# Layer 0 of a four-layer convolution stack: PSUM in two-bank tiles with one reader each, and a 128-column stationary for one image half

## The chip, the core and the metric

The kernel runs on one core of a Trainium2 chip. A core has TensorE (PE: matmuls, with the loading of stationary operands shown as PEld), VectorE (DVE), ScalarE (ACT), GpSimd (POOL, used here mostly to issue stores) and SyncE (SP, used to issue loads). Matmuls write PSUM, which has eight banks of 512 fp32 values in each of 128 partitions; ACT and DVE read PSUM and write SBUF. The metric is the device time of one execution in microseconds: 6857.07 us, the median of three runs (6852.17 to 6867.05).

## What is computed

The input x has the shape (4, 64, 256, 256) in fp32. Four layers follow one another, each of the form `x = x + conv(group_norm(x))`. Only layer 0 is touched:

```python
x = jnp.einsum('bchw,oc->bohw', x, w_in)            # 64 -> 384 channels
xp = x.reshape(B, C, H // p, p, W // p, p)...       # patches of 8 x 8
xp = irfft2(rfft2(xp) * fft_filter)                 # per channel and patch
x = conv_general_dilated(x, w_dw, 3 x 3, depthwise)
x1, x2 = jnp.split(x, 2, axis=1)
x = gelu(x1) * x2
return jnp.einsum('bchw,oc->bohw', x, w_out)        # 192 -> 64 channels
```

Layers 1 to 3 are a 3x3 convolution, a gated 1x1 convolution and a spectral convolution.

## The kernel before

Layer 0 treats the 64 pixels of a patch as the partition index of what it computes. The FFT filter and the depthwise 3x3 convolution are folded, at the start, into per-channel matrices from the 64 pixels of a patch (and of its right, lower and lower-right neighbours) to the pixels of an output patch. The image is cut into 12 blocks `p` of up to 12 patch rows, three per image; each block is worked in four channel blocks `kb` of 96 expanded channels (48 for each side of the gate). For each `kb` three kinds of work run on TensorE:

- Expansion, `expand(p, kb, t)`, once for each patch row `t` (11 or 12 of them; 544 tiles in the whole kernel). SBUF tile `xn` holds a normalised patch row: input channels of the left image half on partitions 0 to 63, of the right half on 64 to 127. A patch's 64 channels x 64 pixels are the stationary operand and the weights `win` (96 columns) the moving one, so the pixels come out on partitions and the channels along the free axis. `k` and `m` count eight pairs of patches, `s` the image half, `odd` the patch of a pair: 32 matmuls of 64x64 with 96 columns. The even patch of a pair goes to partitions 64 to 127 and the odd one to 0 to 63, with `win` read from column 48 or 0, so that one copy of 128 partitions can move both gate sides. The result is read by two ACT copies (L452, L455) and two DVE copies (L456, L457) into the big SBUF tile `u`.
- Convolution, `convolve(p, kb, g)`, twelve per `kb` (576 in all): per-channel matmuls of the folded matrices `w` with `u`, first 64x64 ones (L488), then 64x16, 64x28 and 64x4 ones (L497) that accumulate the neighbours' part. ACT applies Gelu to the first gate side (L504), DVE multiplies by the second (L505), POOL stores the product to DRAM (`gs`).
- Projection, `project(p - 1, r)`, for the block before: `g` is loaded back with channels on partitions and multiplied by `w_out` (L588 with 128x64, L595 with 64x64 tiles); DVE adds the residual `rt` (L603, L605) and takes the statistics for the next group norm (L611), POOL stores (L615). Eight units `r` per block; one runs after the expansions of each `kb` and one in the middle of its convolutions. `unit()` calls `project`, then `load_unit` for the next `r`.

All of layer 0's PSUM comes from `quad`: two tiles of four banks, used in turn by the three kinds of work and by the small matmuls of the group norms:

```python
def quad(name):
    return pp.tile([128, 4, 512], F32, tag=f"p{next(turn) % 2}", name=name)
```

The order on TensorE, ACT, DVE and SP is the order in which the program issues the work (`tc.manual_schedule`); a tile is reused when all its readers are done. The weights `w` are loaded by `load_w` into a ring of three tiles, two ahead. The other loads on SP are the next block's input rows, the statistics of the next image and the projection's operands. The constants `c_ident`, `c_avg32` and `c_sel32`, which only later layers read, are loaded at the very start.

Of the kernel before, what the change touches and what calls it, by code (L numbers as in the profile page):

```python
# [17 lines left out]
C = 64  # L18
HID = 192
# [102 lines left out]
class _Net:  # L122
    def __init__(self, ctx, tc, a):
# [10 lines left out]
        self.ident = self.load("c_ident")  # L134
        self.avg = self.load("c_avg")
        self.avg32, self.sel32 = self.load("c_avg32"), self.load("c_sel32")
# [30 lines left out]
    def stats_tile(self, name, n):  # L167

        return self.sp.tile([128, self.H // 2, 6], F32, tag="bst", name=name)[:, 0:n]
# [107 lines left out]
    def _layer0(self, ctx, dst):  # L277
# [5 lines left out]
        def quad(name):  # L283

            return pp.tile([128, 4, 512], F32, tag=f"p{next(turn) % 2}", name=name)

        self.small = lambda name: quad(name)[:, 0, :]
# [23 lines left out]
        p_w, p_h = pool("l0w", 3), pool("l0h", 4)  # L311
# [122 lines left out]
        def expand(p, kb, t):  # L434

            b, i0 = blocks[p]
            ps = quad(f"psu_{p}_{kb}_{t}")
            xn = xns[b, i0 + t]
            for k in range(2):
                for m in range(4):  # L440
                    for s in range(2):
                        for odd in range(2):
                            nc.tensor.matmul(  # L443
                                ps[halves[1 - odd], 2 * s + k, 2 * PB * m : 2 * PB * (m + 1)],
                                xn[halves[s], 2 * (4 * k + m) + odd].rearrange("p r w -> p (r w)"),
                                win[halves[s], kb, PB * (1 - odd) : PB * (3 - odd)], start=True, stop=True,
                            )
            v = ps[:, :, 0 : 8 * PB].rearrange("p s (m c) -> p c s m", m=4)
            n = 4 * 4
            at = lambda h, o: u[h, :, t * CW + o : t * CW + o + n].rearrange("p c (s m) -> p c s m", s=4)  # L450
            first, second = v[:, 0:PB], v[:, PB : 2 * PB]
            nc.scalar.copy(at(slice(0, 128), 1), first)  # L452
            lo, hi = halves
            k = PB * 7 // 12
            nc.scalar.copy(at(hi, E2 + 1)[:, 0:k], second[lo, 0:k])  # L455
            nc.vector.tensor_copy(at(lo, O1), second[hi])  # L456
            nc.vector.tensor_copy(at(hi, E2 + 1)[:, k:], second[lo, k:])  # L457
# [21 lines left out]
        def convolve(p, kb, g):  # L479

            ps = quad(f"pc_{p}_{kb}_{g}")
            G = NG * kb + g
            w = wl[p * (HID // 8) + G // 2]
            out = lambda lo, m, k, h: ps[lo : lo + m, 2 * k + h, 0:L].rearrange("p (i x j) -> p i x j", i=NR, x=2)
# [18 lines left out]
            v = ps.rearrange("p (k h) n -> p h k n", h=2)[:, :, :, 0:L]  # L503
            nc.scalar.activation(h, v[:, 0], AF.Gelu)  # L504
            nc.vector.tensor_mul(h, h, v[:, 1])  # L505
# [51 lines left out]
        def load_unit(p, r):  # L557
            if p < 0 or p >= NB:
                return
            load_r(p, r)  # L560
            for half in range(2):
                load_g(p, r, half)

        def project(p, r):
# [4 lines left out]
            po = quad(f"po_{p}_{r}")  # L569
            rt = rts.pop((p, r))  # L570
# [12 lines left out]
            for half in range(2):  # L583
                g1, g6 = loads.pop((p, r, half))
                for k in range(2):
                    for x in range(2):
                        for s in range(2):
                            nc.tensor.matmul(  # L588
                                out(2 * half + k, s, x), wo1, moving(g1[:, 2 * k], 2 * half + k, s, x),
                                start=(x == 0), stop=False, skip_group_check=True,  # L590
                            )
                for x in range(2):
                    for k in range(2):
                        for s in range(2):
                            nc.tensor.matmul(  # L595
                                out(2 * half + k, s, x), wo6[halves[k]],
                                moving(g6[halves[k], 0], 2 * half + k, s, x),
                                start=False, stop=True, tile_position=(k * C, s * C), skip_group_check=True,
                            )
            rv = rt.rearrange("p i (j w) -> p w (i j)", w=P)  # L600
            pv = po[:, :, 0 : 2 * n].rearrange("p b (k n) -> p b k n", k=2)
            v = rv[:, 1:7].rearrange("p (b k) n -> p b k n", k=2)
            nc.vector.tensor_add(v, v, pv[:, 0:3])  # L603
            v = bass.AP(tensor=rv.tensor, offset=rv.offset + 7, ap=[rv.ap[0], [-7, 2], rv.ap[2]])
            nc.vector.tensor_add(v, v, pv[:, 3])  # L605
# [28 lines left out]
        with ordered:  # L634
# [30 lines left out]
            for j in range(2):  # L665
                load_w(j)
# [19 lines left out]
            for p in range(NB + 1):  # L686
                units = iter(range(P if p > 0 else 0))
# [5 lines left out]
                for r in range(ahead):  # L693
                    load_unit(p - 1, r)

                def unit():
                    r = next(units, None)
                    if r is None:
                        return
                    project(p - 1, r)  # L700
                    if r + ahead < P:
                        load_unit(p - 1, r + ahead)

                if p == NB:
                    for r in range(P):
                        unit()
# [771 lines left out]
```

## Time and profile before

| What | Value |
|---|---|
| median of three runs | 6857.07 us |
| profiled execution, its own time | 6889.14 us |
| span of the profiled execution | 6887.4 us |
| mean granted TensorE clock | 0.938 |
| PE busy | 5931.4 us (86%) |
| DVE busy | 3944.2 us (57%) |
| ACT busy | 2973.2 us (43%) |
| POOL busy | 1049.0 us (15%) |
| last store of layer 0 issued | about 4315 us after the start |

A group line of the profile reads: source line, engine, operation, output and inputs by the program's names, for matmuls the stationary's rows and columns, shapes, count; then busy time in us and the mean of one in ns; then the engine's idle time just before these instructions and what ended most of it. A timeline line gives the start and length in us, and in square brackets the idle time before it and its releaser. A window line gives a stretch, its length, the busy time and number of instructions of PE, PEld, DVE, ACT and POOL, the granted TensorE clock (1.00 is full), the share of the DMA engines and GB/s. An fp32 matmul appears as two weight loads and two matmuls (two passes). The ends of matmuls are modelled; their starts are records.

### The profile page before, as it was taken

The numbers are of one execution on the slowest core, as the hardware profiler recorded it, in microseconds if no ns is written. First come the engines' busy times: TensorE is split into PE (matmuls) and PEld (weight loads), VectorE is DVE, ScalarE is ACT, GpSimd is POOL, SyncE is SP. The second block draws the span as 40 slices with busy tenths as digits, with TensorE's granted clock in tenths as the row PEclk, the third lists the DMA queues.
The fourth block names the chain that finished last, engine by engine and source line by source line (L and its number), as shares of the span: only waits on it lengthen the run. The fifth ranks groups of instructions, "written<-read, shape, count | busy, mean of one in ns | idle before, by whom it ended". The sixth has DMA issues, their size and how long they took to land.

```text
span 6887.4 us, 252749 instructions
## 1 busy us (share of the span) xinstructions
PE 5931.4 (86%) x115416; PEld 3078.3 (45%) x115416; DVE 3944.2 (57%) x4436; ACT 2973.2 (43%) x3172; POOL 1049.0 (15%) x1646
## 2 busy tenths in 40 slices
PE   2888888888888888888888886999989999999987
PEld 1444444444444444444444443333344444444476
DVE  5444444444444444444444443899888889886355
ACT  3332323233323233323333330677777777774211
POOL 3111111111111111111111111111112222221011
PEclk9999999999999999999999997999999999999855
DMA  7577878786878777878676769999957667667889
GB/s 223 147 195 195 216 200 213 198 204 196 216 202 213 196 210 198 212 197 216 190 201 185 193 175 223 240 229 227 227 134 175 167 173 173 177 168 250 330 341 391
DMA packets 878558, 1448.60 MB, mean 210 GB/s; under 512 B 77252, under 2 KB 586452, under 8 KB 875444
## 3 DMA queue, kind: packets, MB, share of 16 engines
q1 hardware_dynamic: 725284, 923.09, 53.6%
q0 software_dynamic: 148672, 500.14, 21.5%
q8 instruction: 909, 14.89, 1.0%
q10 hardware_dynamic: 3536, 9.20, 0.5%
q14 instruction: 157, 1.29, 0.1%
HBM read 932.08 MB, written 500.04 MB: 208 GB/s over the span
## 4 chain that ended last, share of the span: by engine, by line
PE 66%; DMA 14%; ACT 6%; DVE 5%; issue 5%; SPq 4%; POOL 0%; ACTq 0%; DVEq 0%; POOLq 0%
PE pc L497 13%; PE m L863 10%; PE pc L488 9%; PE psu L443 8%; PE one L1104 8%; PE div L1063 6%; DMA w<-wt 4%; DMA g<-g 4%; PE po L588 3%; ACT u L452 3%; DMA x<-x 2%; PE psz L1093 2%; SPq L544 2%; PE po L595 2%; ACT u L455 2%
## 5 line engine op out<-in xcount | busy, mean ns | idle before, releaser
L443 PE MATMUL psu<-win,xn 64*64 64x96 f32 x34816 | 934.2, 260 | 495.1 <-DVE u L457 303.6
L504 ACT ACTIVATE h<-pc 128x748 f32<-128x748 f32 x576 | 457.1, 794 | 2033.6 <-PE pc L497 2033.6
L505 DVE TENSOR_TENSOR h<-h,pc 128x748 f32<-128x748 f32 x576 | 535.8, 931 | 1273.9 <-ACT h L504 1273.9
L497 PE MATMUL pc<-u,w 64*16 64x374 f32 (+2 forms) x27648 | 1263.1, 489 | 0.7 <-issue 0.7
L443 PEld LDWEIGHTS psu<-win,xn 64*64 64x64 f32 x34816 | 842.5, 144 | 606.8 <-issue 254.0
L488 PE MATMUL pc<-u,w 64*64 64x374 f32 x9216 | 896.9, 498 | 119.3 <-DMA w<-wt 88.8
L456 DVE COPY u<-psu 64x768 f32<-64x768 f32 x544 | 522.0, 960 | 687.7 <-ACT u L455 637.5
L497 PEld LDWEIGHTS pc<-u,w 64*16 64x16 f32 (+2 forms) x27648 | 415.8, 93 | 788.6 <-issue 787.8
L452 ACT COPY u<-psu 128x768 f32<-128x768 f32 x544 | 461.7, 849 | 668.6 <-PE psu L443 664.5
L508 POOL DMA_DIRECT2D g<-h x576 | 416.1, 722 | 1728.7 <-DVE h L505 1636.8
L1049 DVE TENSOR_TENSOR q<-xn 128x2313 f32<-128x2313 f32 (+2 forms) x256 | 627.9, 2495 | 1.7 <-ACT xn L258 1.7
L1104 PE MATMUL one<-z,wp 32*32 32x512 f32 x16384 | 595.1, 597 | 21.1 <-issue 17.7
L488 PEld LDWEIGHTS pc<-u,w 64*64 64x64 f32 x9216 | 325.4, 134 | 623.8 <-issue 483.8
L258 ACT ACTIVATE xn<-x,nb,r 128x1024 f32<-128x1024 f32 (+3 forms) x272 | 485.5, 1788 | 180.9 <-DMA x<-x 142.8
L1050 ACT ACTIVATE q<-q 128x2313 f32<-128x2313 f32 (+2 forms) x256 | 529.0, 2086 | 30.0 <-DVE q L1049 29.0
L1063 PE MATMUL div<-q,ones 64*32 64x512 f32 x8192 | 474.0, 602 | 12.2 <-ACT q L1050 9.3
L1104 PEld LDWEIGHTS one<-z,wp 32*32 32x32 f32 x16384 | 368.6, 103 | 228.7 <-issue 86.9
L615 POOL DMA_DIRECT2D x<-r x192 | 148.4, 777 | 1872.7 <-DVE r L605 1555.1
L1137 POOL DMA_DIRECT2D x<-r x512 | 274.8, 545 | 981.1 <-DVE r L1134 965.9
L588 PE MATMUL po<-g,wo 128*64 128x176 f32 (+1 forms) x3072 | 315.3, 348 | 97.1 <-DMA g<-g 56.9
L603 DVE TENSOR_TENSOR r<-r,po 128x1056 f32<-128x1056 f32 (+1 forms) x96 | 198.1, 2064 | 321.1 <-PE po L595 295.8
L863 PE MATMUL m<-t,wk 64*64 64x512 f32 x3072 | 341.1, 588 | 0.0
(155 smaller groups left out, 6009.5 us busy)
## 6 DMA issues: line engine op xcount, KB each, us to landing
g<-h POOLq DMA_DIRECT2D x576, 374.0 KB, 7.5
x<-x SPq DMA_DIRECT2D x240, 640.0 KB, 6.5
w<-wt SPq DMA_DIRECT2D x288, 448.0 KB, 8.3
x<-x SPq DMA_DIRECT2D x100, 1024.0 KB, 14.1
g<-g SPq DMA_DIRECT2D x414, 187.0 KB, 5.9
g<-g SPq DMA_DIRECT2D x736, 93.5 KB, 5.8
x<-in_x_dram SPq DMA_DIRECT2D x256, 256.0 KB, 9.5
x<-o POOLq DMA_DIRECT2D x128, 512.0 KB, 8.4
```

The source lines that it names most:

```text
L443: nc.tensor.matmul(ps[halves[1 - odd], 2 * s + k, 2 * PB * m : 2 * PB * (m + 1)], xn[halves[s], 2 * (4 * k + m) + odd].rearrange("p r w -> ...
L452: nc.scalar.copy(at(slice(0, 128), 1), first)
L456: nc.vector.tensor_copy(at(lo, O1), second[hi])
L488: nc.tensor.matmul(out(C * c, C, k, h), w[halves[h], k, 2 * (G % 2) + c, 0:C], cells(h, 4 * g + 2 * k + c, 0, 0), start=True, stop=False, ...
L497: nc.tensor.matmul(out(q, m, k, h), w[halves[h], k, 2 * (G % 2) + c, c0 : c0 + m], cells(h, 4 * g + 2 * k + c, down, right), start=False, ...
L505: nc.vector.tensor_mul(h, h, v[:, 1])
L588: nc.tensor.matmul(out(2 * half + k, s, x), wo1, moving(g1[:, 2 * k], 2 * half + k, s, x), start=(x == 0), stop=False, skip_group_check=True,)
L863: nc.tensor.matmul(rows2(m)[halves[j], s], w[dx][halves[s]], ts[n][halves[s], i, 2 * j : 2 * j + 2, dx : dx + W], start=(dx == 0), stop=(d ...
L1049: nc.vector.tensor_sub(d, p0, p1)
L1050: nc.scalar.activation(d, d, AF.Square)
L1063: ins = nc.tensor.matmul(ps[quarters[j], h], ones[halves[h]], q[n, g, k][halves[h], r + 2 * j : r + 2 * j + 2, o : o + W], start=(m == 0), ...
L1104: ins = nc.tensor.matmul(rows2(ps[g])[quarters[j], k], w[quarters[i]], z[quarters[i], h, 2 * j + dy : 2 * j + dy + 2, dx : dx + W], tile_p ...
```

## The change

PSUM in layer 0 becomes four tiles of two banks (`banks`) in place of two of four. An expansion takes two of them: the left image half fills one, which only ACT reads (four copies of 64 partitions), the right half the other, which only DVE reads (three copies). For the left half, the two patches of a pair form one stationary of 64 rows and 128 columns; the right half keeps its 64x64 matmuls. The two kinds alternate: one of the first, two of the second, eight times. A convolution takes two tiles, one for each `k`, and Gelu and product are issued for each. A projection unit is cut into two halves of one tile each, run after the convolutions 1, 4, 7 and 10 of a `kb`; loads follow by halves (`load_half`). The ring of `w` has four tiles, loaded three ahead. The statistics tile is shorter, three constants are loaded after layer 0, and the group-norm step after the last convolution of a `kb` is skipped. The core of the diff:

```diff
-        def quad(name):
-            return pp.tile([128, 4, 512], F32, tag=f"p{next(turn) % 2}", name=name)
-        self.small = lambda name: quad(name)[:, 0, :]
+        def banks(name):
+            return pp.tile([128, 2, 512], F32, tag=f"p{next(turn) % 4}", name=name)
+        self.small = lambda name: banks(name)[:, 0, :]
...
-        p_w, p_h = pool("l0w", 3), pool("l0h", 4)
+        p_w, p_h = pool("l0w", 4), pool("l0h", 4)
...
         def expand(p, kb, t):
-            ps = quad(f"psu_{p}_{kb}_{t}")
+            ps = [banks(f"psu_{p}_{kb}_{t}_{s}") for s in range(2)]
+            lo, hi = halves
+            both = win[lo, kb, 0 : 2 * PB]
             for k in range(2):
                 for m in range(4):
-                    for s in range(2):
-                        for odd in range(2):
-                            nc.tensor.matmul(
-                                ps[halves[1 - odd], 2 * s + k, 2 * PB * m : 2 * PB * (m + 1)],
-                                xn[halves[s], 2 * (4 * k + m) + odd].rearrange("p r w -> p (r w)"),
-                                win[halves[s], kb, PB * (1 - odd) : PB * (3 - odd)], start=True, stop=True,
-                            )
...
+                    n, at = 2 * (4 * k + m), slice(2 * PB * m, 2 * PB * (m + 1))
+                    nc.tensor.matmul(
+                        ps[0][:, k, at], xn[lo, n : n + 2].rearrange("p n r w -> p (n r w)"), both, start=True, stop=True
+                    )
+                    for odd in range(2):
+                        nc.tensor.matmul(
+                            ps[1][halves[1 - odd], k, at], xn[hi, n + odd].rearrange("p r w -> p (r w)"),
+                            win[hi, kb, PB * (1 - odd) : PB * (3 - odd)], start=True, stop=True,
+                        )
...
-            nc.scalar.copy(at(slice(0, 128), 1), first)
-            nc.scalar.copy(at(hi, E2 + 1)[:, 0:k], second[lo, 0:k])
-            nc.vector.tensor_copy(at(lo, O1), second[hi])
-            nc.vector.tensor_copy(at(hi, E2 + 1)[:, k:], second[lo, k:])
+            for h, o, k, c in ((lo, O1, lo, 0), (hi, O2, lo, PB), (lo, E1 + 1, hi, 0), (hi, E2 + 1, hi, PB)):
+                nc.scalar.copy(at(h, o), v[0][k, c : c + PB])
+            nc.vector.tensor_copy(at(slice(0, 128), 8 + 1), v[1][:, 0:PB])
+            nc.vector.tensor_copy(at(hi, 8 + E2 + 1), v[1][lo, PB:])
+            nc.vector.tensor_copy(at(lo, 8 + O1), v[1][hi, PB:])
...
-            nc.scalar.activation(h, v[:, 0], AF.Gelu)
-            nc.vector.tensor_mul(h, h, v[:, 1])
+            for k in range(2):
+                nc.scalar.activation(h[:, k], ps[k][:, 0, 0:L], AF.Gelu)
+                nc.vector.tensor_mul(h[:, k], h[:, k], ps[k][:, 1, 0:L])
...
-        def project(p, r):
+        def project(p, r, half):
-            po = quad(f"po_{p}_{r}")
+            po, rt = banks(f"po_{p}_{r}_{half}"), rts[p, r]
...
-                    unit()
                     for g in range(NG):
-                            load_w(p * (HID // 8) + G // 2 + 2)
+                            load_w(p * (HID // 8) + G // 2 + 3)
                         convolve(p, kb, g)
-                        self.next_norms()
-                        if g == NG // 2:
+                        if g < NG - 1:
+                            self.next_norms()
+                        if g in (1, 4, 7, 10):
                             unit()
...
     net.layer0(x1)
+    late = ctx.enter_context(tc.tile_pool(name="late", bufs=1))
+    net.ident, net.avg32, net.sel32 = (net.load(name, late) for name in ("c_ident", "c_avg32", "c_sel32"))
```

## The prediction

> **What bounds the kernel now.** I read the groups by cost first, then the timeline of one expansion and one convolution stage, then the granted clock by window, and last the start records of all matmuls. "Slower" and "faster" below mean by more than 0.2%, about what a measurement of this kernel tells from no change.
>
> Layer 0 lasts to about 4312 us. Its rows:
>
> ```profile
> L443 PE MATMUL psu<-win,xn 64*64 64x96 f32 x34816 | 934.2, 260 | 495.1 <-DVE u L457 303.6
> L497 PE MATMUL pc<-u,w 64*16 64x374 f32 (+2 forms) x27648 | 1263.1, 489 | 0.7 <-issue 0.7
> L456 DVE COPY u<-psu 64x768 f32<-64x768 f32 x544 | 522.0, 960 | 687.7 <-ACT u L455 637.5
> L452 ACT COPY u<-psu 128x768 f32<-128x768 f32 x544 | 461.7, 849 | 668.6 <-PE psu L443 664.5
> L488 PE MATMUL pc<-u,w 64*64 64x374 f32 x9216 | 896.9, 498 | 119.3 <-DMA w<-wt 88.8
> ```
>
> The 544 expansion tiles (L443, two records per fp32 matmul) wait for their readers; the convolutions (L488, L497) wait for almost nothing. Summed over the start records, the 48 expansion stretches take 1451 us (2.67 us a tile), the convolutions 2222 us, the projections 521 us. One tile of a stretch, in order of time:
>
> ```profile
> 1052.30 1.58 PE L443 MATMUL psu<-win,xn 64*64 64x96 f32 x64 [1.01 <-ACT u L452]
> 1053.97 0.85 ACT L452 COPY u<-psu 128x768 f32<-128x768 f32 x1 [1.18 <-PE psu L443]
> 1054.85 0.53 ACT L455 COPY u<-psu 64x448 f32<-64x448 f32 x1
> 1055.41 0.96 DVE L456 COPY u<-psu 64x768 f32<-64x768 f32 x1 [1.12 <-ACT u L455]
> 1056.38 0.48 DVE L457 COPY u<-psu 64x320 f32<-64x320 f32 x1
> ```
>
> ACT, then DVE, read the one tile in turn: fill 1.6, reading 3.1 us with the gaps, two tiles in flight, so about 2.35 us a tile; TensorE itself needs 1.6. This chain is what the change opens. But look at what TensorE does when the shape of its tiles changes (convolution, TensorE alone):
>
> ```profile
> 1003.46 1.46 PE L488 MATMUL pc<-u,w 64*64 64x374 f32 x16
> 1004.85 2.14 PE L497 MATMUL pc<-u,w 64*16 64x374 f32 x48
> ```
>
> L488 uses 64x64 tiles, L497 64x32. Within a shape, four L443 matmuls start within 20 ns and the next four 82.5 ns later: 96 columns take 80 ns (374 take 312), all tiles stream at once, weights load behind. At a change of shape nothing overlaps. In 551 of the 576 changes L488 to L497 the first new matmul starts 410 to 413 ns after the last old one of *any* tile: 312 of stream plus 100. It stands on rows 0-63, yet from the last matmul on its own rows the gap varies, 426 to 452; so it waits for the other row half too. The change between 64 and 128 columns (L1291 to L1306, gap 523 less 427) costs 96.
>
> **The change, part by part.** (a) *Evacuation split.* The two-bank tiles give ACT four copies of 64x384 and DVE one of 128x384 and two of 64x384. From 849 ns at 768 and 529 at 448 elements ACT has 81 + 1.0 per element: 4 x 465 = 1.86 us. DVE (960 at 768, 484 at 320) has 144 + 1.06: 3 x 552 = 1.66 us. In parallel, so reading falls from 3.1 to about 1.9 us.
>
> (b) *Filling.* The built order is, eight times per tile, one 64x128 matmul on rows 0-63, then two 64x64 ones on rows 64-127: 24 matmuls in place of 32, but 16 changes of shape. For each, the new weights' load is exposed. 64 columns: L443's second round after a change comes at 133 ns instead of 82.5, so 51 to 53. 128 columns: the L205 pair,
>
> ```profile
> 1446.20 0.30 PEld L205 LDWEIGHTS gn<-mv,sb_c_avg 128*128 128x128 f32 x2 [1.18 <-issue]
> ```
>
> whose two loads start 109 ns apart and whose one-column matmuls end 111 ns apart; L1438's first 32x128 matmul lasts 104 longer than the next. I take 107 per load. The two passes of the 64x128 matmul share one tile: load 107, second load 107 (beside the first stream), stream 80, change 96 = 390 ns. The two 64x64 tiles run beside each other: 133 to the second pass, 7 for the second tile, 80, 96 = 316. Together 706 ns, 5.65 us a tile. ACT and DVE are then hidden wholly under TensorE; should the changes cost nothing, ACT's 1.86 comes out again.
>
> (c) *Clock.* The trace grants full or half clock in windows of 3.41 us:
>
> ```profile
> 5159.10:5162.50 3.40, 3.40 (x101) 1.90 (x77) 3.40 (x3) 3.40 (x3) 0.00 (x0) 1.00 1.03 217
> 5162.50:5165.90 3.40, 1.74 (x29) 0.49 (x35) 3.40 (x2) 3.06 (x2) 0.00 (x0) 1.00 0.73 137
> 5165.90:5169.30 3.40, 3.40 (x48) 1.08 (x34) 3.40 (x3) 1.09 (x1) 0.00 (x0) 0.50 0.28 56
> ```
>
> (first PE busy, later PEclk). After the half-used middle window the clock halves. I worked out each window's used share of the array: every matmul's stream time times its tile's rows and columns over 128x128. After 150 us: of 71 full-clock windows under 0.33, 67 were followed by half clock; of 1618 over 0.385, none. From half clock all 77 windows over 0.76 led back to full, of 152 under 0.70 only 4. Time alone sorts worse: that middle window had matmuls streaming 45% of the time, a share of 0.25. The new expansion streams half the array for 320 of 706 ns, a share of 0.23. So after one or two windows it should run at half clock and stay (0.27 there).
>
> Half-clock prices: change 132 ns (L488 to L497, 18 cases, gap 756 less 623); after a change L443's second round at 215; a 128-column load 163 exposed (L1438, 792 against 629), and the L205 pair's ends 215 apart. 64x128: 163 + 215 + 160 + 132 = 670; 64x64: 215 + 7 + 160 + 132 = 514. 1184 ns, 9.47 us a tile. The expansion: 544 x 9.47 = 5152, less 146 for some 4.5 us of each of 48 stretches at full clock (0.80 instead of 0.48 tile): 5006 us, +3555.
>
> (d) *Rule against row.* The trace's rule above has the clock fall without any idle stretch: in the middle window the longest gap was 1.66 us. The Trainium skill, "TensorE: Matmul & The Clock Gate", section "What's actually happening", has the half rate come back after an idle window of about 3.4 us; the new expansion has no such gap, and by that rule the time would be 8340 us, by the trace's share 10310. I go by the trace.
>
> (e) *Convolutions* keep their matmuls. Their reading is split by k: ACT 2 x 0.45 and DVE 2 x 0.55 us, under the 3.5 us of TensorE per convolution: nothing. The cover has 3.5 - (0.16 + 0.9 + 0.55) = 1.9 us of slack; a projection's adds and statistics, queued on DVE ahead of the product, hold it for 2.1 + 0.8 + 1.75 us today, and after the change for 1.4 us, then 0.8 + 0.8 + 1.75 us three convolutions later. TensorE waits little for that today (23.6 us on L505 at L488), so between 0 and -24; I take 0. At the end of each stretch the convolution starts at half clock for about 4 us: +96, against about 48 that it loses today.
>
> (f) *Queues.* On SP the weights w are asked for three pairs ahead instead of two and a stretch grows by 70 us: the 88.8 us of waits on w go. g is loaded by halves after each half projection, its DMAs as many, spread between w's loads: of L588's 97 us of idle I take 30 away (bounds 0 and 60). Half projections between convolutions save a change of shape or two per unit: -15 (0 to -30). POOL's stores are the same. The three constants leave the head of SP for the head of layer 1: three issues of 0.5 us, +2 (0 to +10).
>
> Sum against the profiled execution (span 6887.4, 6889.1 with what lies around it): 6887 + 3555 + 48 - 89 - 30 - 15 + 2 = 10358, 10360 with the rest. That execution is 0.47% over the median 6857.07; scaled by 0.9953: 10310 us. Own bounds of this sum: the second load fully beside the first stream at half clock, 9.03 us a tile, and a window more at full clock, 10000; a 64-column load of 107 instead of 54 at half clock, in both passes, 10750.
>
> **Rivals.** *Clock stays full* (weight loads or mere occupancy counting as use): 544 x 5.65 = 3074, span 8378, scaled 8340 us. For it: matmuls follow without idle gaps; against it: 71 windows.
>
> *Row halves do not wait for each other* (faster): 64x128 and 64x64 lie on disjoint rows and write different banks. Then eight steps of two 107 ns loads fill a tile in 1.7 us; with 0.3 to the first read, 1.94 of copies and 0.14 back the two buffers turn a tile in 2.05 us: 1115 + 96 for 48 starts = 1211, 240 less than now, scaled 6490 us. It decides if a step costs under 0.33 us (2.67 / 8). Against it stands the constant gap of 410 to 413; that pair covers both halves with each shape, and no row shows two shapes on disjoint rows. The Trainium skill, "TensorEngine Tiling (Array Packing)", section "Key Properties", lets a change of mode drain the whole engine.
>
> *Worse:* if the two 64x64 tiles did not stream beside each other (L443's four and L588's two do), each step would grow by two streams, 320 ns at half clock, 2.56 us for each of some 520 tiles: 1330 more, scaled 11640 us.
>
> **Chances.** Drain with half clock 0.70, drain with full clock 0.14, no drain 0.12, worse still 0.04. Faster 0.12, within 0.2% 0.01, slower 0.87. The range 8250 to 10900 holds the first two; the likeliest alone is 10000 to 10800.
>
> **What would show it.** Right: expansion stretches of about 105 us; in them, TensorE's idle time put down to its own issue at each 64x128 load; half clock through them in the clock row and full in the convolutions; ACT and DVE waiting for psu, not TensorE for them; no waits on w. Wrong: the 64x64 matmuls start within 20 ns of the 64x128 ones, or the clock row stays at 9 through layer 0.

## The result and the profile after

The changed kernel takes 10415.8 us (median of four runs, 10405.3 to 10430.0) against 6862.1 us for the kernel before on the same chip: a ratio of 1.517, 95% interval 1.513 to 1.522. The profiled execution took 10405.3 us, span 10403.5.

The busy rows, the clock row and the shares of the chain by engine, from the page of the changed kernel:

```profile
PE 10048.6 (97%) x106712; PEld 5569.6 (54%) x106712; DVE 4126.4 (40%) x5652; ACT 3379.1 (32%) x4836; POOL 1052.1 (10%) x1646
...
PEclk9667676676676676675666766757669999999975
...
PE 93%; DMA 3%; DVE 1%; issue 1%; ACT 0%; POOL 0%; SPq 0%; DVEq 0%; POOLq 0%; ACTq 0%
```

TensorE looks busy from end to end, with fewer matmuls than before, and the clock row lies between 5 and 7 through layer 0 (the first three quarters, without the first slice): 4674 of the 5010 us of expansion went by at half clock. The groups of the changed kernel that answer to the five shown of before (L442 and L446 stand for L443; L453 is the line of ACT's four copies, L454 the first of DVE's three; L487 and L496 are the convolutions):

```profile
L442 PE MATMUL psu<-win,xn 64*128 64x96 f32 x8704 | 3112.6, 458 | 12.1 <-ACT u L453 6.7
L442 PEld LDWEIGHTS psu<-win,xn 64*128 64x128 f32 x8704 | 2089.8, 297 | 976.5 <-issue 918.1
L446 PE MATMUL psu<-win,xn 64*64 64x96 f32 x17408 | 2477.0, 382 | 0.0
L453 ACT COPY u<-psu 64x384 f32<-64x384 f32 x2176 | 1116.3, 513 | 3872.9 <-PE psu L442 3833.5
L454 DVE COPY u<-psu 128x384 f32<-128x384 f32 x544 | 303.7, 558 | 4075.8 <-PE psu L446 4057.7
...
L496 PE MATMUL pc<-u,w 64*16 64x374 f32 (+2 forms) x27648 | 1275.6, 493 | 0.4 <-issue 0.2
...
L487 PE MATMUL pc<-u,w 64*64 64x374 f32 x9216 | 989.0, 516 | 53.5 <-DVE u L456 52.8
```

Who waits for whom has turned round. Before, TensorE stood idle for 495 us ahead of the expansion. For 360 of them it waited for the copies of ACT and DVE, and 102 were put down to its own issue (total, times, longest):

```profile
PE psu L443 <- DVE u L457: 303.6, 274, 23.6
PE psu L443 <- issue: 101.6, 72, 4.4
```

Now ACT and DVE wait 3834 and 4058 us for TensorE, and TensorE waits 12 us there in all. The convolutions nearly keep their means (493 ns against 489, 516 against 498), and they have no wait on `w` left.

The timeline of the changed kernel, TensorE alone, within one expansion stretch:

```profile
1549.73 0.58 PE L446 MATMUL psu<-win,xn 64*64 64x96 f32 x4
1550.24 0.74 PE L442 MATMUL psu<-win,xn 64*128 64x96 f32 x2
1550.91 0.58 PE L446 MATMUL psu<-win,xn 64*64 64x96 f32 x4
1551.42 0.74 PE L442 MATMUL psu<-win,xn 64*128 64x96 f32 x2
```

From one start of L442 to the next 1.18 us: 0.67 for the 64x128 matmul with its change of shape, 0.51 for the two 64x64 ones with theirs. The same stretch by windows (length, then busy time of PE, PEld, DVE, ACT, POOL, then the granted clock; it starts at 1512.57):

```profile
1500.00:1520.00 20.00, 20.00 (x280) 10.41 (x272) 9.93 (x18) 4.96 (x12) 4.47 (x6) 0.95 1.03 327
1520.00:1540.00 20.00, 20.00 (x104) 13.29 (x103) 3.53 (x7) 4.25 (x9) 0.00 (x0) 0.50 0.45 93
1540.00:1560.00 20.00, 20.00 (x103) 13.29 (x103) 3.34 (x6) 4.11 (x8) 0.00 (x0) 0.50 0.01 2
```

The clock halves within a few microseconds and stays there, while PE counts as busy all the time.

Where the time went, from the start records of all matmuls of the two profiled executions (us):

| Stretches of | before | after | difference | predicted |
|---|---|---|---|---|
| expansion (48 stretches) | 1451.2 | 5010.4 | +3559.2 | +3555 |
| convolution | 2222.0 | 2213.7 | -8.3 | +48 - 89 = -41 |
| projection | 520.6 | 507.3 | -13.3 | -30 - 15 = -45 |
| the rest of the kernel | 2693.6 | 2672.0 | -21.6 | +2 |
| span | 6887.4 | 10403.5 | +3516.1 | +3471 |

The expansion alone makes the loss. What remained to be tested is why: whether the changes of shape make it or the 128-column stationary, the split reading or the moved loads; and what sets the clock.

### The profile page after: what moved, and what is told of

Same layout as the page of the kernel before. It is cut to its first block, busy times and chain, and to the rows that moved or that the text cites. A ratio compares the mean times of both kernels' runs of the same rounds, so it can differ in the third digit from the quotient of the medians.

```text
span 10403.5 us, 238266 instructions
## 1 busy us (share of the span) xinstructions
PE 10048.6 (97%) x106712; PEld 5569.6 (54%) x106712; DVE 4126.4 (40%) x5652; ACT 3379.1 (32%) x4836; POOL 1052.1 (10%) x1646
## 4 chain that ended last, share of the span: by engine, by line
PE 93%; DMA 3%; DVE 1%; issue 1%; ACT 0%; POOL 0%; SPq 0%; DVEq 0%; POOLq 0%; ACTq 0%
PE psu L442 27%; PE psu L446 21%; PE pc L496 12%; PE pc L487 8%; PE m L862 6%; PE one L1103 6%; PE div L1062 4%; PE po L584 3%; PE po L591 1%; PE psz L1092 1%; PE psa L1290 1%; DMA x<-x 1%; DMA g<-g 1%; PE psy L1437 1%; PE zero L1103 1%
## 5 line engine op out<-in xcount | busy, mean ns | idle before, releaser
L442 PE MATMUL psu<-win,xn 64*128 64x96 f32 x8704 | 3112.6, 458 | 12.1 <-ACT u L453 6.7
L442 PEld LDWEIGHTS psu<-win,xn 64*128 64x128 f32 x8704 | 2089.8, 297 | 976.5 <-issue 918.1
L446 PE MATMUL psu<-win,xn 64*64 64x96 f32 x17408 | 2477.0, 382 | 0.0
L453 ACT COPY u<-psu 64x384 f32<-64x384 f32 x2176 | 1116.3, 513 | 3872.9 <-PE psu L442 3833.5
L454 DVE COPY u<-psu 128x384 f32<-128x384 f32 x544 | 303.7, 558 | 4075.8 <-PE psu L446 4057.7
L446 PEld LDWEIGHTS psu<-win,xn 64*64 64x64 f32 x17408 | 1227.9, 195 | 718.8 <-issue 688.0
L496 PE MATMUL pc<-u,w 64*16 64x374 f32 (+2 forms) x27648 | 1275.6, 493 | 0.4 <-issue 0.2
L504 DVE TENSOR_TENSOR h<-h,pc 128x374 f32<-128x374 f32 x1152 | 575.1, 541 | 1352.3 <-ACT h L503 1351.3
L503 ACT ACTIVATE h<-pc 128x374 f32<-128x374 f32 x1152 | 492.9, 480 | 1890.9 <-PE pc L496 1887.4
L487 PE MATMUL pc<-u,w 64*64 64x374 f32 x9216 | 989.0, 516 | 53.5 <-DVE u L456 52.8
L496 PEld LDWEIGHTS pc<-u,w 64*16 64x16 f32 (+2 forms) x27648 | 418.8, 94 | 813.8 <-issue 811.7
L487 PEld LDWEIGHTS pc<-u,w 64*64 64x64 f32 x9216 | 360.6, 139 | 532.6 <-issue 379.0
L584 PE MATMUL po<-g,wo 128*64 128x176 f32 (+1 forms) x3072 | 315.8, 349 | 62.3 <-DMA g<-g 39.4
L1136 POOL DMA_DIRECT2D x<-r x512 | 276.3, 551 | 976.9 <-DVE r L1133 950.3
```

Source lines behind the costliest of these rows:

```text
L442: nc.tensor.matmul(ps[0][:, k, at], xn[lo, n : n + 2].rearrange("p n r w -> p (n r w)"), both, start=True, stop=True)
L446: nc.tensor.matmul(ps[1][halves[1 - odd], k, at], xn[hi, n + odd].rearrange("p r w -> p (r w)"), win[hi, kb, PB * (1 - odd) : PB * (3 - od ...
L453: nc.scalar.copy(at(h, o), v[0][k, c : c + PB])
L487: nc.tensor.matmul(out(C * c, C, k, h), w[halves[h], k, 2 * (G % 2) + c, 0:C], cells(h, 4 * g + 2 * k + c, 0, 0), start=True, stop=False, ...
L496: nc.tensor.matmul(out(q, m, k, h), w[halves[h], k, 2 * (G % 2) + c, c0 : c0 + m], cells(h, 4 * g + 2 * k + c, down, right), start=False, ...
L504: nc.vector.tensor_mul(h[:, k], h[:, k], ps[k][:, 1, 0:L])
```

## The experiments

All are edits of the changed kernel, in `expand` unless said otherwise; the diffs show the core of each. In altfull, narrow and rows32 DVE also reads its two banks in four copies, as in both128. Each ratio is to the kernel before, run beside it on the same chip. "Expansion" below is the sum of its stretches in the profiled execution, 5010.4 us in the changed kernel.

**One shape again (same64).** The left half goes back to 64x64; everything else of the change stays.

```diff
-                    nc.tensor.matmul(ps[0][:, k, at], xn[lo, n : n + 2]..., both, start=True, stop=True)
+                    for odd in range(2):
+                        nc.tensor.matmul(ps[0][halves[odd], k, at], xn[lo, n + odd]..., both, start=True, stop=True)
```

> The changed kernel, but the left image half is expanded by two 64x64 matmuls per pair again, into the same places; its four ACT copies, the two-bank tiles and all the rest stay. So the expansion has one tile shape and no change of shape. Theory (the changes of shape make the loss): the clock stays full, TensorE fills a tile in 1.6 us, and ACT's four copies (513 ns each in the changed kernel's profile, 2.05 us) set the pace: 544 x 2.1 + 48 x 2 = 1240 us of expansion in place of 5010, on the 5395 us that the rest took in that profile: 6635 us, about 0.967 of the kernel before. Rival (the split reading or the moved loads and projections make the loss): it stays near 10400. Rival between (the split reading costs something too): anything over 6860.

Measured: 6787.1 us, ratio 0.988 (0.985 to 0.990). The loss is gone, so neither the split reading, nor the two-bank tiles, nor the moved loads make it. But the gain is a third of what I expected: expansion 1483 us in place of 1240. That miss is taken up with the run named three.

**128 columns on both halves (both128).** One shape again, now the other one.

```diff
-                    for odd in range(2):
-                        nc.tensor.matmul(ps[1][halves[1 - odd], k, at], xn[hi, n + odd]..., win[hi, kb, ...], ...)
+                    nc.tensor.matmul(ps[1][:, k, at], xn[hi, n : n + 2]..., win[hi, kb, 0 : 2 * PB], ...)
...
-            nc.vector.tensor_copy(at(slice(0, 128), 8 + 1), v[1][:, 0:PB])
-            nc.vector.tensor_copy(at(hi, 8 + E2 + 1), v[1][lo, PB:])
-            nc.vector.tensor_copy(at(lo, 8 + O1), v[1][hi, PB:])
+            for h, o, k, c in ((lo, O1, lo, 0), (hi, O2, lo, PB), (lo, E1 + 1, hi, 0), (hi, E2 + 1, hi, PB)):
+                nc.vector.tensor_copy(at(h, 8 + o), v[1][k, c : c + PB])
```

> The changed kernel, but the right image half is expanded with 128-column stationaries as well (eight 64x128 matmuls per half), and DVE reads its two banks in four copies like ACT's. One shape again, and twice as many 128-column loads. Theory (a change of shape is what costs, a 128-column load is 107 ns): if the loads of the two row halves run beside each other, 8 x 2 x 107 ns = 1.71 us fill a tile and DVE's four copies set the pace, 2.25 us: 544 x 2.25 + 96 = 1320, 6715 us in all; if the loads run one after another, 3.42 us a tile and a share of the array of 0.37, which should just keep the clock: 1960, 7355 us; at half clock 4.9 us a tile at most, 8060. Rival (the 128-column stationary as such is what costs 0.67 us per matmul at half clock): 8 x 0.67 = 5.4 us a tile even if both halves run beside each other, 8330 us or more.

Measured: 6616.8 us, ratio 0.963 (0.959 to 0.966); expansion 1298 us. This is the fastest version found and beats both kernels. Its timeline, TensorE alone, in an expansion:

```profile
1539.89 0.27 PE L445 MATMUL psu<-win,xn 64*128 64x96 f32 x1
1539.92 0.27 PE L442 MATMUL psu<-win,xn 64*128 64x96 f32 x1
1540.00 0.27 PE L445 MATMUL psu<-win,xn 64*128 64x96 f32 x1
1540.04 0.27 PE L442 MATMUL psu<-win,xn 64*128 64x96 f32 x1
```

On each row half a pass starts every 0.11 us, the price of a 128-column load that the prediction took from L205 (107 to 111 ns), and the two halves run side by side, some 40 ns apart. Twice as many of the stationaries that were under suspicion, and less than a third of the time: the 128-column load as such is cheap. What was dear was to alternate it with another shape.

**The same matmuls, grouped (group8).** Eight 64x128, then sixteen 64x64: two changes of shape per tile in place of sixteen.

```diff
             for k in range(2):
                 for m in range(4):
                     n, at = 2 * (4 * k + m), slice(2 * PB * m, 2 * PB * (m + 1))
                     nc.tensor.matmul(
                         ps[0][:, k, at], xn[lo, n : n + 2].rearrange("p n r w -> p (n r w)"), both, start=True, stop=True
                     )
+            for k in range(2):
+                for m in range(4):
+                    n, at = 2 * (4 * k + m), slice(2 * PB * m, 2 * PB * (m + 1))
                     for odd in range(2):
```

> The changed kernel with the same 24 matmuls per tile in another order: first the eight 64x128 ones, then the sixteen 64x64 ones. Two changes of shape per tile in place of sixteen. Theory: at full clock 390 + 7 x 214 + 316 + 7 x 165 = 3.36 us a tile, with the array used to a share of 0.38, just above where windows of both traces lost the full clock (none over 0.385 lost it, most under 0.33 did): 544 x 3.36 + 96 = 1925, 7320 us. If the share is not enough after all, at half clock 670 + 7 x 430 + 514 + 7 x 330 = 6.5 us a tile: 8930 us. Rival (the two operand forms cost by themselves, whatever their order): it stays near 10400. Rival (row halves do not wait for each other, the order on each half is what counts): no difference to 10400 either.

Measured: 7271.5 us, ratio 1.059 (1.055 to 1.063); expansion 1935 us, by the prices 1925. The same 24 matmuls on the same rows in the same program order within each half, and 7 us of the expansion at half clock in place of 4674: within a half the shape never changes, so if a half did not wait for the other, grouping could not have made it faster. The order alone is worth 3075 us of expansion.

**Both halves change together (altfull).** For even `m` both halves by 64x128, for odd `m` both by 64x64, so that eight changes per tile remain.

```diff
+                    if m % 2 == 0:
+                        nc.tensor.matmul(ps[0][:, k, at], xn[lo, n : n + 2]..., both, ...)
+                        nc.tensor.matmul(ps[1][:, k, at], xn[hi, n : n + 2]..., win[hi, kb, 0 : 2 * PB], ...)
+                    else:
+                        for odd in range(2):
+                            nc.tensor.matmul(ps[0][halves[odd], k, at], xn[lo, n + odd]..., both, ...)
+                        for odd in range(2):
+                            nc.tensor.matmul(ps[1][halves[odd], k, at], xn[hi, n + odd]..., win[hi, kb, 0 : 2 * PB], ...)
```

> Both image halves change shape together: for even m both halves by one 64x128 matmul, for odd m both by two 64x64 ones, and DVE reads its banks in four copies. Eight changes of shape per tile in place of sixteen, and each shape streams through the whole height of the array instead of half of it. By the prediction's prices one pair of steps (64x128, then 64x64) takes 390 + 316 + some 10 = 716 ns at full clock and about 1190 at half. Four such pairs make a tile. TensorE streams for 320 of 716 ns, 45% of the time as in the changed kernel, but with a used share of the array of 0.45 in place of 0.23. If the used share sets the clock, it stays full: 544 x 2.86 + 96 = 1652 us of expansion on 5318 for the rest (as in the run with 128 columns on both halves): 6970 us. If the time that anything streams sets it, the clock falls as in the changed kernel (45% there too): 544 x 4.76 = 2590, about 7800 us. If alternating shapes cost nothing when both halves change together: 544 x 2.25 + 96, 6640 us.

Measured: 6978.3 us, ratio 1.018 (1.015 to 1.020); expansion 1639 us against 1652 by the prices at full clock. Less the 96 us for the starts, a pair of steps takes (1639 - 96) / 544 / 4 = 0.71 us, the price worked out from the trace of before at full clock. It also rules out that the mere time in which something streams sets the clock: by the full-clock prices 45% here and 45% in the changed kernel, with opposite clocks (4 us of this expansion at half).

**One tile of the array at a time (onetile).** Only 64x64 stationaries, eight on one tile, then eight on the next: no change of shape, a quarter of the array.

```diff
+            for odd in range(2):
+                for k in range(2):
+                    for m in range(4):
+                        n, at = 2 * (4 * k + m), slice(2 * PB * m, 2 * PB * (m + 1))
+                        nc.tensor.matmul(ps[0][halves[odd], k, at], xn[lo, n + odd]..., both, ...)
+            for odd in range(2):
+                for k in range(2):
+                    for m in range(4):
+                        n, at = 2 * (4 * k + m), slice(2 * PB * m, 2 * PB * (m + 1))
+                        nc.tensor.matmul(ps[1][halves[1 - odd], k, at], xn[hi, n + odd]..., win[hi, kb, ...], ...)
```

> The matmuls of the kernel with 64x64 stationaries on both halves, ordered so that one of the four 64x64 tiles works at a time: eight matmuls on one tile, then eight on the next, and so on. No change of shape, no idle gap over some tenths of a microsecond, but a quarter of the array in use. Theory (the clock follows the used share of the array): share 0.25, so half clock through the expansions, 32 x 2 x 160 ns = 10.2 us a tile: about 5395 + 5570 - 150 = 10800 us, with no change of shape at all. Rival (the clock falls only after an idle window): full clock, 32 x 2 x 80 ns = 5.1 us a tile: 5395 + 2785 + 96 = 8280 us.

Measured: 7684.2 us, ratio 1.119 (1.115 to 1.122); expansion 2380 us. The theory that I had predicted with falls here. Windows view of this kernel within an expansion stretch:

```profile
1542.38:1556.38 14.00, 14.00 (x217) 14.00 (x216) 5.56 (x10) 7.12 (x14) 0.00 (x0) 1.00 0.67 152
```

A used share of cells of 0.30 (0.25 by plan; the last passes on each 64x64 tile of the array overlap the first ones on the next, so an expansion tile takes 4.37 us and not 5.1), and the clock is full. In the kernel before, windows at such a share had lost it.

**Half the columns (narrow).** Each 64x64 stationary of that run cut into two of 32 columns.

```diff
+            for s in range(2):
+                for odd in range(2):
+                    for q in (0, 32):
+                        for k in range(2):
+                            for m in range(4):
+                                n, at = 2 * (4 * k + m), slice(2 * PB * m, 2 * PB * (m + 1))
+                                nc.tensor.matmul(
+                                    ps[s][64 * odd + q : 64 * odd + q + 32, k, at], xn[halves[s], n + odd]...[:, q : q + 32],
+                                    win[halves[s], kb, 0 : 2 * PB], ..., tile_position=(64 * s, 64 * odd + q),
+                                )
```

> One tile of the array at a time again, but each 64x64 stationary cut into two of 32 columns: twice as many matmuls, an eighth of the array in use, something streaming nearly all the time, one shape. The run with one 64x64 tile at a time took 4.37 us per expansion tile with its clock full at a share of 0.30. If the time that anything streams sets the clock, it stays full: 544 x 8.75 + 96 = 4860, on 5318: 10170 us. If the used share does, with its limit for steady work between 0.23 and 0.30, it falls: 544 x 17.5 = 9520, less some 200 for the starts: 14600 us.

Measured: 9878.5 us, one execution; expansion 4572 us, all but 9 us of it at full clock. Cells in use: 0.15. So the share of cells does not set the clock. Two ideas were left: streaming time together with cells, or the rows of the array alone. This run and onetile stream over about half of its rows (0.49 and 0.56 with the overlaps), the changed kernel over 0.24 of them before its clock falls.

**The same share of cells, other streaming time (group2).** Two 64x128, then four 64x64, and so on.

```diff
-                for m in range(4):
+                for m2 in (0, 2):
+                    for m in (m2, m2 + 1):
+                        nc.tensor.matmul(ps[0][:, k, at], xn[lo, n : n + 2]..., both, ...)
+                    for m in (m2, m2 + 1):
+                        for odd in range(2):
+                            nc.tensor.matmul(ps[1][halves[1 - odd], k, at], xn[hi, n + odd]..., win[hi, kb, ...], ...)
```

> The changed kernel's matmuls, alternating in groups of two: two 64x128, then four 64x64, and so on, eight changes of shape per tile. By the prediction's prices 390 + 214 + 316 + 165 = 1085 ns per group pair at full clock, 4.34 us a tile; 7.8 us at half clock. Used share of the array 0.295, as in the run with one tile at a time, but something streams in only 59% of the time, there 98%. If the used share alone sets the clock, with its limit under 0.30, the clock stays full: 544 x 4.34 + 96 = 2460, on 5318: 7780 us. If streaming time counts too, it falls: 544 x 7.8 = 4240, less some 130: 9430 us.

Measured: 9446.3 us, one execution; expansion 4048 us, 3720 of it at half clock. At a share of cells of 0.30, where the run with one tile at a time kept its clock, this one lost it. Again the rows sort them: 0.30 here, 0.56 there.

**Rows against columns (rows32).** As many matmuls as with one 64x64 tile at a time, but with 32 rows and 64 columns each; the sums leave out half of the input channels.

```diff
+                rows = slice(64 * s, 64 * s + 32)
+                nc.tensor.matmul(ps[s][halves[odd], k, at], xn[rows, n + odd]..., win[rows, kb, 0 : 2 * PB], ...)
```

> One tile of the array at a time, as many matmuls of 96 columns as in the run with one 64x64 tile at a time, but each of 32 rows and 64 columns: channels 32 to 63 are left out of the expansion, so the sums run over half of the input channels. That run streamed in 98% of the time over about half of the array's rows and kept its clock (4.37 us a tile); the run with 64x32 tiles kept it too, at an eighth to a sixth of the cells. Theory formed from those two (the clock follows the share of the array's rows that streams, whatever the columns, with its limit near 0.36): here a quarter of the rows, share about 0.28 at most: half clock, 544 x 8.74 = 4755 us less some 150 for the starts, on 5350 for the rest: 9950 us. Rivals (streaming time, or the cells of the array together with the time): no less of both than in the 64x32 run, so full clock, 544 x 4.37 = 2380, on 5300: 7680 us.

Measured: 9547.2 us, one execution; expansion 4184 us, 3855 of it at half clock. Windows view of the 64x32 run, then of the 32x64 run, each within an expansion stretch:

```profile
1620.83:1634.83 14.00, 14.00 (x223) 14.00 (x220) 4.45 (x8) 2.50 (x5) 0.00 (x0) 1.00 0.61 124
```

```profile
1642.26:1656.26 14.00, 14.00 (x117) 14.00 (x115) 4.15 (x8) 4.10 (x8) 0.00 (x0) 0.50 1.18 197
```

Both have an eighth of the cells in one tile, both are busy for 14.00 of 14.00 us, neither has a change of shape. 64 rows by 32 columns keep the full clock, 32 rows by 64 columns lose it, and onetile, with 64 rows and 64 columns, kept it too. Why rows count and columns do not, no run shows. The time was overestimated by 4% (7.7 us a tile and not 8.74), because the last passes on a tile overlap the next tile here as well.

**At the limit (group4).** Groups of four: four changes per tile.

```diff
             for k in range(2):
                 for m in range(4):
                     nc.tensor.matmul(ps[0][:, k, at], xn[lo, n : n + 2]..., both, ...)
+                for m in range(4):
                     for odd in range(2):
                         nc.tensor.matmul(ps[1][halves[1 - odd], k, at], xn[hi, n + odd]..., win[hi, kb, ...], ...)
```

> The changed kernel's matmuls, alternating in groups of four: four changes of shape per tile. By the prediction's prices 390 + 3 x 214 + 316 + 3 x 165 = 1843 ns per pair of groups at full clock, 3.69 us a tile; 670 + 3 x 430 + 514 + 3 x 330 = 3464 ns and 6.93 us at half. Streaming share of the array's rows 0.347: in the windows between 0.33 and 0.35 of the ten traces so far every one (38 of 38) lost the full clock, above 0.39 only 8 of 9673 did. If that limit holds for steady work, half clock: 3770 - 130 us of expansion on 5400: 9040 us. If not (steady work at 0.35 is enough): 544 x 3.69 + 96 = 2100, on 5318: 7420 us.

Measured: 8940.6 us, one execution; expansion 3557 us, 3233 of it at half clock. A share of rows of 0.35 is too little, the 0.38 of group8 is enough.

With that quantity (for each window of 3.41 us, the time in which a row of the array has something streaming over it, averaged over its rows; a matmul's rows taken from its line of the kernel, convolutions and projections counted as using all rows) I sorted the windows of layer 0 in all fourteen traces, from the first recorded fall of the clock in each:

| share of rows | full-clock windows | then half clock |
|---|---|---|
| under 0.33 | 340 | 340 |
| 0.33 to 0.35 | 58 | 58 |
| 0.35 to 0.37 | 68 | 60 |
| 0.37 to 0.39 | 445 | 16 |
| 0.39 and more | 13141 | 9 |

From half clock none of 4673 windows under 0.70 led back to full, 34 of 145 between 0.70 and 0.80, and 459 of 465 above 0.80.

**ACT's fourth copy (three).** 64x64 on both halves, placed so that ACT too needs only three copies.

```diff
-            for h, o, k, c in ((lo, O1, lo, 0), (hi, O2, lo, PB), (lo, E1 + 1, hi, 0), (hi, E2 + 1, hi, PB)):
-                nc.scalar.copy(at(h, o), v[0][k, c : c + PB])
+            nc.scalar.copy(at(slice(0, 128), 1), v[0][:, 0:PB])
+            nc.scalar.copy(at(hi, E2 + 1), v[0][lo, PB:])
+            nc.scalar.copy(at(lo, O1), v[0][hi, PB:])
```

> Both halves by 64x64 matmuls in the placing that the right half has (even patch on partitions 64 to 127, with the weights read from column 48), so that ACT as well as DVE reads its two banks in three copies instead of four. No change of shape. A tile's two buffers then turn in (1.6 to fill + 0.3 to the first read + 1.66 for DVE's three copies + 0.14) / 2 = 1.85 us, and TensorE streams at a share of 0.69: 544 x 1.85 + 96 = 1100, on 5318: 6420 us, 0.935 of the kernel before. Rival (what kept the run with 64x64 on both halves at 1483 us of expansion is not ACT's fourth copy but waiting in bursts with the clock falling in between): some 300 us of half clock remain and the expansion takes about 1350: 6670 us.

Measured: 6723.2 us, ratio 0.980 (0.978 to 0.982); expansion 1445 us, 313 of it at half clock. The rival holds in kind: to do without the fourth copy was worth 39 us of expansion, and TensorE still waits; the rival's own 1350 us was 95 too low. What TensorE waits for, the waits of this kernel's TensorE over one stretch (1146 to 1172 us) and its timeline say:

```profile
PE psu L448 <- issue: 5.6, 2, 4.2
PE psu L443 <- ACT u L457: 0.4, 1, 0.4
```

```profile
1152.48 0.29 PE L448 MATMUL psu<-win,xn 64*64 64x96 f32 x1 [1.38 <-issue]
1155.27 0.38 PE L443 MATMUL psu<-win,xn 64*64 64x96 f32 x4 [0.35 <-ACT u L457]
1160.26 0.42 PE L448 MATMUL psu<-win,xn 64*64 64x96 f32 x2 [4.19 <-issue]
```

In the middle of a tile TensorE stands still for 1.4 and 4.2 us, and the profile names no engine and no data transfer that releases it. The trace also records the blocks of 16 KB that the instruction queue brings in (a fetch of 1.1 us, median). Of the 179 gaps over 0.5 us from one start to the next inside expansion tiles of this kernel, 364 us in sum, 165 end between 1.1 and 1.7 us after such a block has landed; a moment picked at random within the expansions falls there one time in nine. The kernel with one shape of 64x64 and four copies has 144 such gaps (289 us, 138 of them after a block), the kernel before 69 (118 us, 66 of them). With 128 columns on both halves there are 5 (3 us), and with one tile at a time 1. The page of three, then that of both128, on this queue (packets, MB, share of 16 engines):

```profile
q8 instruction: 911, 14.93, 1.0%
```

```profile
q8 instruction: 775, 12.70, 0.8%
```

Spread over TensorE's loads and matmuls (230832 in three, 196016 in both128) these are 65 bytes each in both kernels, so the queue seems to bring TensorE's instructions. A tile of 64x64 matmuls takes 128 records of loads and matmuls in as little as 1.3 us of filling, a tile with 128 columns on both halves takes 64 in 1.7 us at its fastest, and the one-tile run 128 in 4.2 us. So the gaps come where instructions are used up fastest, and nearly all end shortly after a block's arrival. Each gap then lowers the share of rows in its window, and 313 us of this expansion are at half clock. No run changed the fetching itself, so that it makes the gaps is not shown: it rests on the coincidence in time and on the three rates.

**The ring of w (both128_b and both128_w3).** The fastest version once more, and the same with three tiles of `w` loaded two pairs ahead.

```diff
-        p_w, p_h = pool("l0w", 4), pool("l0h", 4)
+        p_w, p_h = pool("l0w", 3), pool("l0h", 4)
...
-            for j in range(3):
+            for j in range(2):
...
-                            load_w(p * (HID // 8) + G // 2 + 3)
+                            load_w(p * (HID // 8) + G // 2 + 2)
```

> The kernel with 128-column stationaries on both halves once more, as the partner of the next run: 6617 us within 0.5%, 0.963 of the kernel before.

> The same with the ring of weights w set back to three tiles, loaded two pairs ahead. Theory (the fourth tile is what removed the waits on w, 88.8 us in the kernel before): these waits come back, between 60 and 90 us, since the stretches are shorter than before: 6680 to 6710 us, about 0.975 of the kernel before. Rival (other changes of the loads removed them): no difference, 6617 us.

Measured: 6605.8 us, ratio 0.962 (0.961 to 0.964), and 6674.4 us, ratio 0.972 (0.970 to 0.974): 69 us for the fourth tile. TensorE's idle time put down to `w` at L485 comes back with 47 us, and the convolutions' time at half clock rises from 32 to 132 us; their stretches grow by 88 us in the profiled executions. The theory holds, and here the waits cost more than their length, the clock falling with them.

## Why the prediction was right, point by point

The predicted 10310 us is 1.0% under the measured 10416, inside the range and inside the likeliest case's own.

- (a) Reading: right in kind, hidden as said. ACT's copies take 513 ns and not 465, so 2.05 us a tile; DVE's 551 to 560 ns were predicted at 552. Both lie under 9.2 us of TensorE. One reading of before was too simple: the tiles were said to wait for their readers, but 102 of the 495 us of idle time stood under "issue", and the run named three ties such gaps, by their timing, to the instruction queue rather than to the copies.
- (b) Changes of shape: right, and the step that decided. A pair of steps takes 0.67 + 0.51 = 1.18 us, predicted 670 + 514 = 1184 ns. The full-clock prices, which the changed kernel never shows for long, come out in the run where both halves change together (1639 us against 1652) and in the run grouped by eight (1935 against 1925). That the halves wait for each other was inferred from a constant gap of 410 to 413 ns in a pair that covers both; group8 shows it directly.
- (c) Clock: right for this kernel, with the wrong quantity. The share of the array was counted in cells, rows times columns. In the changed kernel every matmul phase covers all 128 columns of half the rows, so the share of cells and that of rows are the same 0.23, and in the kernel before nothing told them apart. The runs onetile and narrow, at 0.30 and 0.15 of the cells with a full clock, show that step to be wrong as a rule; rows32 shows what stands in its place. That the term came out right was luck to that extent: the same rule gave 10800 us for onetile, which took 7684. The limit, between 0.33 and 0.385 in the prediction, is between 0.35 and 0.38 of the rows.
- (d) The Trainium skill, "TensorE: Matmul & The Clock Gate", section "What's actually happening", has the half rate return after an idle window of about 3.4 us. The runs decide against that as a full account: rows32 loses the clock while TensorE is busy for 14.00 of 14.00 us, its matmuls starting at most 0.22 us apart within the expansions but for a single wait, and 340 of 340 windows fall under a share of rows of 0.33. By that rule the prediction put the time at 8340 us.
- (e) Convolutions: mis-sized. At half clock they spend 284.7 us in place of 113.7, which costs about 85 us, where +48 was taken; that is 5.9 us for each of the 48 stretches on average and not 4.
- (f) Queues: the waits on `w` are gone as said, and both128_w3 confirms what removed them, but at the start of each stretch the first convolution now waits for the last copies instead: 52.8 us for DVE's at L487, and 95.2 us of its weight loads for ACT's. So -89 was not all to be had. The projection's idle time ahead of L584 is 62.3 us against 97.1, 35 us less where 30 were taken; but the projection stretches shrank by 13 us and not by 45, and where the rest went stays open.
- The sum: the terms together missed by 45 us. Convolutions and projections, (e) and (f), came out 33 and 32 us above their terms and the expansion 4; the rest of the kernel came out 24 us below its term, which stays unexplained. Another 49 us come from scaling the sum by 0.9953: the profiled execution of before was long by 0.47%, and I carried that over, but the changed kernel's profiled execution lies 0.1% under its own median, which makes up the last 10 us.

The rivals: full clock (8340) falls with the clock row. Independent row halves (6490) fall with group8. 64x64 tiles that do not stream beside each other (11640) fall with the 0.51 us per step. The Trainium skill's "TensorEngine Tiling (Array Packing)", section "Key Properties", has a change of mode drain the engine; the runs agree and add the price: two changes with the matmuls between them took 0.71 us at full clock (altfull) and 1.18 us at half.

## What to carry to other kernels

Keep one tile shape on TensorE within a stretch, on both row halves at once: a second shape on disjoint rows was not parallel work here but a drain, and regrouping the same matmuls moved this kernel from 10416 to 7271 us. Count the share of the array's rows that stream in a window of 3.4 us: under about 0.36 the clock halved here whatever the columns did, and only a window above 0.7 to 0.8 brought it back, so a pattern that falls once stays down. A wider stationary was worth having here once both halves had it and the number of matmuls halved: 128 columns on both halves gave 0.962 of the kernel before.

## What the runs showed of the hardware beyond that

- The rows of the array, not its cells and not TensorE's busy time, went with the clock: 64x32 tiles one at a time kept it at 0.15 of the cells, 32x64 tiles lost it.
- TensorE at 64x64 with 96 columns stood still inside tiles: 118 us of gaps in the kernel before, 289 and 364 in the two runs that read the tiles faster, nearly all of them ending 1.1 to 1.7 us after a 16 KB block of the instruction queue landed. The profile calls these gaps "issue"; that instructions were used up faster than they came is inferred from these times.
- 64-column loads are hidden on a single tile too: in the one-tile run consecutive passes on one tile start 82 to 83 ns apart, the time that 96 columns take, while with 128-column stationaries on both halves the passes on one row half start 111 to 112 ns apart.
